# Constant tiles, second-layer weights and token transposes in the last stage of a four-stage transformer kernel

## The chip, the cores and the metric

The kernel runs on one core of one Trainium2 chip. The metric is the device time of one execution, in microseconds (us). Of the kernel before the change three runs are shown; the median counts.

A core has a matrix engine (TensorE, PE in the profile; its weight loads are PEld), a vector engine (VectorE, DVE), an activation engine (ScalarE, ACT), a general one (GpSimd, POOL), and a queue engine that here only issues DMAs (SyncE, SP). They run side by side; each executes its own instructions in order. SBUF is the memory on the core, with 128 partitions; PSUM is the matrix engine's output memory, here used as eight banks of 128 x 512 float32.

## What is computed

Two batches of 1024 tokens with 128 features pass four blocks in a row, each added to its input after a layer norm:

```python
x = x + _layernorm(_L0_attn_ref(_layernorm(x), Wq, Wk, Wv))      # 8 heads, full softmax attention
x = x + _layernorm(_L0_ffn_ref(_layernorm(x), ...))              # 8 experts, top 2, and a shared one
x = x + _layernorm(_L1_attn_ref(_layernorm(x), ...))             # 16 heads of 8, causal, ALiBi bias
x = x + _layernorm(_L1_ffn_ref(_layernorm(x), ...))              # two layers, below
```

The last block is a small transformer of its own, and the change lies in it. One layer of it (8 heads of 64, windows of 64 tokens, hidden size 341):

```python
h = shift_token(x)                 # second half of the features comes from the token before
q, k, v = jnp.split(h @ wqkv, 3, axis=-1)
q = l2norm(q) * qs
k = l2norm(k) * ksc
q, k = rotary_xpos(q, k)
o = local_attention(q, k, v)       # each window of 64 sees itself and the window before
x = x + o @ wo
h = shift_token(x)
h = (h - mu) / jnp.sqrt(var + 1e-05) * lg + lb
a, g = jnp.split(h @ w1 + b1, 2, axis=-1)
x = x + (a * jax.nn.gelu(g)) @ w2 + b2
```

## The kernel before

One function per block, `phase1` to `phase4`, written as generators. The tokens stay in SBUF in X, 16 tiles of 128 tokens (8 for each batch). Float32 products are made of halves: a value is split into a high and a low part (`split_r`, L214 and L215: a cast on ACT and a subtraction on DVE), and `mm3` (L49 to L51) multiplies them in three matmuls.

**What sets the order.** A framework with a planner compiles the program. The planner runs the program on a simulated timeline and gives each engine, whenever it comes free, the earliest instruction of the text that is ready there. PE alone is bound to the order of the text inside the fourth stage, by `in_line`, which chains its instructions. ACT's functions that need a table of their own (Ln, Exp, Gelu) are chained under the key "tables", and `k.last["tables"]` is the newest of them. `issue_after(ins)` puts what is written inside it behind `ins`; the third stage's `tick` enters it with four instructions, one each of ACT, DVE, SP and POOL.

**Third stage (`phase3`).** Steps of 4 heads by up to 512 queries by 128 keys. PE computes scores twice: in a pass ahead that only finds row maxima (L856, L860 on PE, L865 on DVE), and again (L891, L893) for the exponentials (L894, ACT, into pt). Of every second step pt is split into hl: a cast on ACT (L898) and a subtraction on POOL (L899). PE then multiplies pt or hl with V (L916, into pu). kz, the masked keys, is made on POOL (L836) and DVE (L838). The last token tiles go through L937 to L958 and the layer norm (L81 to L117) into X at L210.

**Preparation of the fourth stage.** From step m >= 54 on, each step of the third stage ends with `k.tick`, which runs `phase4` up to its next `yield`, behind the newest exponential, maximum, DMA and kz instruction. So the constants of pool p4c (`cp`: mask, identb, pick, away, fac), `normalize(0)` (the layer norm of batch 0 into F[0]: statistics on DVE at L81, L82 and L84, the power on POOL at L88, the application on DVE at L92), `weights(0)` and the first `stage_x` lie beside the third stage. `weights` loads a matrix through SP, scales it on POOL (L1041), casts it on ACT (L1043), subtracts on POOL (L1044), scales the rotary table on POOL in four parts (L1057) and a column (L1066).

**Fourth stage (`phase4`).** After "main" the pools p4e (`ep`, working tiles), p4w (`wp`) and p4s (`sp`) are opened. p4w holds F1 (batch 1), K0 to K4, V0 to V5, Vs0 to Vs5, xm, and the constants sh (the matrices that shift tokens), Z0 and Z1 (a zeroed pair of buffers into which half of q is cast), mz0 and mz1, and mT0 to mT2. They are filled at L1130 (sh, by SP), L1135 (mT, by three DMAs of POOL), L1137 and L1138 (memsets of Z and mz on POOL) and L1140 (the ones column of V). p4w lies where the third stage still has data: its first writes come after X's last write.

The work is 32 tiles of 128 tokens (2 layers x 2 batches x 8 tiles), in a software pipeline: round i of the loop does the steps of several tiles, in the order of

```python
for step in ("b0", "a2", "b2", "c2", "a", "e1", "d", "a1", "gated", "f", "x", "c", "gated", "e", "b1"):
```

each for tile i minus its lateness, (0, 0, 1, 2, 2, 2, 3, 4, 4, 4, 5, 6) for a, a1, a2, b0, b1, b2, c, c2, d, e, e1, f. What they do:

- x (every fourth round): `transposed` turns four token tiles into one PSUM bank (L221, PE), `split_r` splits it into hTh and hTl, the second half of the features shifted by one token, and at the first half of a batch the last column into xc.
- a: q and k by `mm3` from hTh and hTl into two banks; a square on ACT, the rotary products rot and t2 on DVE (L1174, L1177). a1: their sum on POOL (L1183), sums of squares (L1185, L1186). a2: the reciprocal norm on ACT and DVE.
- b0: q and k are scaled on POOL (L1208) and cast on ACT, q also into Z. b1: the low halves (L1222 DVE, L1223 POOL), and three transposing DMAs of SP: Z to Qz (L1229), k16 to K (L1230), q16 to Q (L1231). b2: v by `mm3` and its copy into V on ACT, then DMAs into Vs (L1245, L1247).
- c: high scores, the mask at L1258 and Qz times K at L1263, and the negated maximum into mz (L1272, DVE); ACT scales K into the next K (L1277). c2: mz transposed on PE (L1283) and copied to mT.
- d: mT and the scores (L1297, L1301, L1302), the exponential (L1303). e: PV (L1314) and the division (L1323, L1324). e1: transposes (L1331) and a copy (L1333). f: the output matrix (L1342) and the sum into F (L1343).
- g (the feed-forward part, several tiles at once): a generator, one part of which runs at each "gated".

Layer 2's `weights` are such a generator too; it is appended at i == 12, and uses pool p4v, opened at i == 2.

PSUM: one bank `ps_sm` (tile name sm), taken in turn by stage_x and stage_c2, and a ring of seven (tile name b, from three pools of 3, 3 and 1), which `bank()` goes round. `SRC` says for some steps whether they take the one or the other.

Of the kernel before, what the change touches and what calls it, by code (L numbers as in the profile page):

```python
# [10 lines left out]
F32 = mybir.dt.float32  # L11
F32R = mybir.dt.float32r
F16 = mybir.dt.float16
# [16 lines left out]
class Core:  # L30
# [7 lines left out]
    def pool(self, name, bufs, side, **kw):  # L38
        return self.tc.tile_pool(name=name, bufs=bufs, side=side, reuse_waits="tile", **kw)
# [956 lines left out]
def phase4(k, X):  # L996
# [5 lines left out]
    nc, A = k.nc, k.A  # L1002
    H, HD, HID = 8, 64, 341
    WS = 256.0
    with ExitStack() as es:
        pool = lambda name, bufs: es.enter_context(k.pool(name, bufs, "right"))
        cp = pool("p4c", 1)
        ps_sm = k.ps_sm
# [14 lines left out]
        fac = cp.tile([128, NT], F32, name="fac")  # L1023
        nc.sync.dma_start(fac, A["c_fac"])

        F = [cp.tile([128, NT, D], F32, name="F0")]

        def normalize(b):
            x = [X[:, NT * b + t, :] for t in range(NT)]
            mv, rstd = k.ln_stats(cp, lambda t: x[t])  # L1030
            yield
            k.ln_to(cp, [F[b][:, t, :] for t in range(NT)], lambda t: x[t], mv, rstd, scalar=b == 1)

        W = {}

        def weights(l, own, work):

            def split(pool, name, shape, dt, src, **kw):
                w = work(shape)
                nc.sync.dma_start(w, src)  # L1040
                nc.gpsimd.tensor_scalar(w, w, WS, None, ALU.mult)  # L1041
                h, lo = pool.tile(shape, dt, name=name + "h"), pool.tile(shape, dt, name=name + "l")
                nc.scalar.copy(h, w)  # L1043
                nc.gpsimd.tensor_tensor(lo, w, k.f(h) if dt == F32R else h, ALU.subtract)  # L1044
                return h, lo

            wq = split(own, "wq", [128, 1024], F16, A["L1_ffn_wqkv"][l][:, 0:1024])
            yield
            wv = split(own, "wv", [128, 512], F16, A["L1_ffn_wqkv"][l][:, 1024:1536])
            yield  # L1050

            qs = own.tile([128, 2, 2, HD], F32, name="qs")
            nc.sync.dma_start(qs, A["t_qks"][l].partition_broadcast(128))
            tab = own.tile([128, 4, NT, HD], F32, name="tab")
            nc.sync.dma_start(tab, A["c_rope"].rearrange("j (t p) d -> p j t d", p=128))
            for j in range(4):
                nc.gpsimd.tensor_tensor(tab[:, j], tab[:, j], qs[:, j // 2, j % 2, :].unsqueeze(1).to_broadcast([128, NT, HD]), ALU.mult)  # L1057
            yield
            wo = own.tile([128, 4, D], F32, name="wo")
            nc.sync.dma_start(wo, A["L1_ffn_wo"][l].rearrange("(a p) d -> p a d", p=128))  # L1060
            w2 = own.tile([128, 3, D], F32, name="w2")
            nc.sync.dma_start(w2, A["t_f2"][l])
            w1 = split(own, "w1", [128, 6, D], F16, A["t_f1"][l])
            col = own.tile([128, 9], F32, name="col")
            nc.sync.dma_start(col, A["t_col4"][l])
            nc.gpsimd.tensor_scalar(col[:, 0:3], col[:, 0:3], WS, None, ALU.mult)  # L1066
            W[l] = *wq, wo, *w1, w2, col, tab, *wv
# [3 lines left out]
        xc = [[cp.tile([128, 1], F16, name=f"xc{b}{n}") for n in "hl"] for b in range(B)]  # L1071
        late_half = slice(64, 128)

        def stage_x(l, b, c):

            hTh = cp.tile([128, 512], F16, name="hTh", bufs=2)
            hTl = cp.tile([128, 512], F16, name="hTl", bufs=2)
            ps = k.transposed(ps_sm, F[b], c)
            k.split_r(hTh[0:64, :], hTl[0:64, :], ps[0:64, :])
            k.split_r(hTh[late_half, 1:512], hTl[late_half, 1:512], ps[late_half, 0:511])  # L1080
            for h, x in zip((hTh, hTl), xc[b]):
                nc.scalar.copy(h[late_half, 0:1], x[late_half] if c else k.zero[late_half])
            if c == 0:
                k.split_r(xc[b][0][late_half], xc[b][1][late_half], ps[late_half, 511:512])
            S["h", l, b, c] = hTh, hTl
# [6 lines left out]
        yield from normalize(0)  # L1092
        yield from weights(0, cp, work0)
        stage_x(0, 0, 0)
        yield "main"

        ep = pool("p4e", 2)
        sq_place = k.acc.rearrange("p (j h) (e d) -> p j (h e) d", j=2, e=2)
        wp = pool("p4w", 1)
        F.append(wp.tile([128, NT, D], F32, name="F1"))  # L1100
        sp = pool("p4s", 2)
        ps = [es.enter_context(k.psum(f"p4{n}", b)) for n, b in zip("xyz", (3, 3, 1))]
# [11 lines left out]
                t = t.bitcast(F16)  # L1114
            return t[:, :shape[1]]
        from_sm = lambda shape, dt: ps_sm.tile(shape, dt, name="sm")
        SRC = {'c2': 0, 'f': 1, 'g': 1, 'x': 0}
        src_c2 = from_bank if SRC["c2"] else from_sm
        src_f = from_bank if SRC["f"] else from_sm
        src_g = from_bank if SRC["g"] else from_sm  # L1120
        src_x = FromBank if SRC["x"] else ps_sm
        QB = 3
        RV = 6
        RK = 5
# [1 line left out]
        V = [wp.tile([128, H, HD + 1], F32, name=f"V{i}") for i in range(RV)]  # L1126
        Vs = [wp.tile([128, H, HD + 1], F32, name=f"Vs{i}") for i in range(RV)]
        xm = [wp.tile([128, 64], F32, name=f"xm{b}") for b in range(B)]
        sh = wp.tile([128, 2, 128], F32, name="sh")
        nc.sync.dma_start(sh, A["c_shift"])  # L1130
        Z = [wp.tile([128, 4, 256], F16, name=f"Z{i}") for i in range(2)]
        mz = [wp.tile([128, 128], F16, name=f"mz{i}") for i in range(2)]
        mTs = [wp.tile([128, 128], F16, name=f"mT{i}") for i in range(3)]
        for m in mTs:
            nc.gpsimd.dma_start(m, A["c_rows4"][int(m is mTs[2])])  # L1135
        for i in range(2):
            nc.gpsimd.memset(Z[i], 0.0)  # L1137
            nc.gpsimd.memset(mz[i], 0.0)  # L1138
        for i in range(RV):
            nc.gpsimd.memset(V[i][:, :, HD : HD + 1], WS)  # L1140

# [5 lines left out]
        def cpy(n, dst, src, i=8):  # L1147
            (nc.scalar.copy if engine(n, i) == "a" else eng(n, i).tensor_copy)(dst, src)
# [52 lines left out]
        def stage_b0(i):  # L1201
# [11 lines left out]
            cpy("kh", ends(k16), pair4(kk), i)  # L1213
            cpy("z", ends(Z[i % 2]), pair4(q))
            S["b", i] = rot, q16, k16

        def stage_b1(i):
# [10 lines left out]
            fl = lambda ap: ap.rearrange("p a n -> p (a n)")  # L1228
            nc.sync.dma_start_transpose(Qz, fl(Z[i % 2]))  # L1229
            nc.sync.dma_start_transpose(K[k0][:, :, 64:192], fl(k16))  # L1230
# [105 lines left out]
        def stage_f(i):  # L1336
# [4 lines left out]
            for a in range(4):  # L1341
                nc.tensor.matmul(ps, oT[:, a, :], wo[:, a, :], start=a == 0, stop=a == 3)  # L1342
            nc.vector.tensor_tensor(F[b][:, t, :], ps, F[b][:, t, :], ALU.add)  # L1343

        def stage_g(l, b, t0, T, last):

            w1h, w1l, w2, col = W[l][3:7]
            x = F[b]
            g = slice(t0, t0 + T)
# [65 lines left out]
            for i in range(T):  # L1415
                nc.tensor.transpose(ps[:, i, :], yT[:, 128 * i : 128 * i + 128], k.ident)
            nc.vector.tensor_tensor(F[b][:, g, :], x[:, g, :], ps, ALU.add)
            if l == 1:
# [16 lines left out]
        gens = []  # L1435

        def advance():
            gens[:] = [g for g in gens if k.in_line(next, g, 0) is None]

        i = 0  # L1440
        while i < 32 + late[-1] or gens:
            if i == 4:
                gens.append(normalize(1))
            if i == 2:
                own = es.enter_context(k.pool("p4v", 1, "right"))
            if i == 12:
                gens.append(weights(1, own, lambda shape: ep.tile(shape, F32, name="t2")))
            for step in ("b0", "a2", "b2", "c2", "a", "e1", "d", "a1", "gated", "f", "x", "c", "gated", "e", "b1"):
                if step == "gated":
                    advance()  # L1450
                elif step == "x":
                    n = i - late[-1]
                    if n in ENDS:
                        l, b, t = where(n)
                        T = n - ([-1] + ENDS)[ENDS.index(n)]
                        gens.append(stage_g(l, b, t - T + 1, T, n >= LAST))
                    if i % 4 == 3 and i + 1 < 32:
                        l, b, t = where(i + 1)
                        k.in_line(stage_x, l, b, t // 4)
                else:  # L1460
                    j = names.index(step)
                    if 0 <= i - late[j] < 32:
                        k.in_line(stages[j], i - late[j])
            i += 1
# [3 lines left out]
def tile_kernel(ctx: ExitStack, tc: tile.TileContext, A, out, first=1, last=4):  # L1468
# [33 lines left out]
    k.exp_tables()  # L1502
    k.later = []
    gens = [f(k, X) for f in (phase1, phase2, phase3, phase4)[first - 1 : last]]
    ready = [False] * len(gens)

# [138 lines left out]
```

## Time and profile before

| | us |
|---|---|
| median of 3 runs | 1388.4 |
| lowest, highest | 1385.42, 1388.5 |
| the profiled execution | 1389.02 |
| its span, first to last instruction | 1387.2 |

| engine | busy us | share of the span |
|---|---|---|
| PE | 1159.8 | 84% |
| DVE | 1045.9 | 75% |
| ACT | 973.0 | 70% |
| POOL | 863.2 | 62% |

In the profiled execution L360, the first stage's attention, runs until 442 us; the third stage's score matmuls (L891) run until 991, X's last write (L210) ends at 1022.87, and the fourth stage's score matmuls (L1263) begin at 1029.4 and end at 1346.8. The granted clock of PE was 0.936 of full speed on average, and 0.54 between 1010 and 1040 us.

How to read the lines that follow. The chain of work that ended last is followed back from the last instruction, at each step to what released it; its rows give start, length, and engine, tile and line. "Issue" is time in which an engine waited for nothing that the profile shows. A timeline row gives start, length, engine, line, operation and tiles, output <- inputs, with partitions x elements and type; xN is the number of instructions in a row that are taken together, and the bracket is the engine's idle time before them and what ended it. A row of waits says who waited, for which instruction, for how long in all, how often, and the longest. DMA_DIRECT2D on POOL or SP is the issuing of a DMA, and DMA_TRANSPOSE that of a transposing one.

### The profile page before, as it was taken

Reading aid. Unit: us, or ns where it says so; the run is one execution under the profiler, and the core shown is the slowest. Engines: PE = TensorE matmul, PEld = TensorE weight load, DVE = VectorE, ACT = ScalarE, POOL = GpSimd, SP = SyncE. Lnnn points to the kernel's source line nnn. Section 1 sums busy time; section 2 is a strip of 40 time slices with the busy share of each in tenths; the row PEclk is TensorE's granted clock in tenths of the full one; section 3 lists DMA queues with packets and bytes.
Section 4 is the critical chain, followed back from the end, with each engine's and each line's share of the span. In section 5 each row is a group of like instructions: output and inputs, shape, how many; then the busy total and the mean of one; then the engine's idle time right before and its main releaser. Section 6 shows DMA issues by size and latency. Waiting matters only on the chain.

```text
span 1387.2 us, 28450 instructions
## 1 busy us (share of the span) xinstructions
PE 1159.8 (84%) x11534; PEld 729.5 (53%) x11534; DVE 1045.9 (75%) x2029; ACT 973.0 (70%) x1494; POOL 863.2 (62%) x536
## 2 busy tenths in 40 slices
PE   4789999999889687776998987689648888988986
PEld 1356666666556565544444443344325655655664
DVE  6776666876662688979978889775679887888854
ACT  2777777887667484641888876579757878887755
POOL 1666667777667363744576677576797786666611
PEclk7999999999999898987999999799959999999998
DMA  2000000010000211200000021000077755545530
GB/s 75 1 2 2 2 2 1 2 32 2 2 1 18 74 48 60 81 19 2 5 3 5 6 52 24 12 8 1 5 149 130 128 104 105 99 98 96 102 61 16
DMA packets 122530, 56.75 MB, mean 41 GB/s; under 512 B 105216, under 2 KB 114320, under 8 KB 122400
## 3 DMA queue, kind: packets, MB, share of 16 engines
q1 hardware_dynamic: 119920, 53.53, 18.3%
q8 instruction: 90, 1.47, 0.4%
q10 hardware_dynamic: 1472, 1.09, 0.3%
q0 software_dynamic: 1008, 0.33, 0.2%
q14 instruction: 40, 0.33, 0.1%
HBM read 20.99 MB, written 1.11 MB: 16 GB/s over the span
## 4 chain that ended last, share of the span: by engine, by line
PE 40%; DVE 31%; ACT 14%; POOL 6%; issue 6%; DMA 2%; SPq 0%; POOLq 0%; DVEq 0%; ACTq 0%
DVE mx L865 6%; PE big L360 5%; PE pu L49 4%; PE pu L51 3%; PE pu L50 3%; DVE nm L332 3%; ACT pt L894 2%; PE pu L916 2%; PE big L49 2%; PE big L50 2%; PE big L51 2%; DVE hl L642 1%; PE bankz L856 1%; PE bank L891 1%; DVE F L92 1%
## 5 line engine op out<-in xcount | busy, mean ns | idle before, releaser
L367 POOL TENSOR_TENSOR hl<-p,hl 128x1024 f16<-128x1024 f32 x128 | 273.9, 2143 | 139.0 <-ACT hl L366 110.9
L899 POOL TENSOR_TENSOR hl<-pt,hl 128x2048 f16<-128x2048 f32 (+1 forms) x48 | 164.7, 3435 | 102.3 <-ACT hl L898 58.9
L332 DVE TENSOR_REDUCE nm<-big 128x2 f32<-128x1024 f32 x128 | 155.1, 1219 | 31.9 <-PE big L329 31.1
L364 ACT ACTIVATE p<-big 128x1024 f32<-128x1024 f32 x128 | 130.8, 1022 | 51.9 <-PE big L360 51.1
L49 PEld LDWEIGHTS <-hl 128*128 128x128 f16 x1024 | 100.5, 98 | 73.8 <-DVE acc L392 41.2
L366 ACT CAST hl<-p 128x1024 f16<-128x1024 f32 x128 | 133.8, 1045 | 4.1
L865 DVE TENSOR_REDUCE mx<-bankz 128x1 f16<-128x512 f32 (+3 forms) x156 | 99.6, 657 | 26.3 <-PE bankz L860 19.5
L894 ACT ACTIVATE pt<-bank 128x512 f32<-128x512 f32 (+1 forms) x173 | 97.3, 601 | 26.0 <-PE bank L893 11.8
L865 DVE TENSOR_REDUCE mx<-bank 128x1 f16<-128x512 f32 (+1 forms) x148 | 94.4, 654 | 18.2 <-PE bank L860 12.5
L1208 POOL TENSOR_TENSOR rot<-rot,rn 128x512 f32<-128x512 f32 x64 | 66.9, 1066 | 61.8 <-DVE rn L1198 44.8
L49 PE MATMUL pu<-V1h,hl 128*128 128x129 f16 x512 | 92.6, 224 | 12.4 <-DVE acc L392 11.1
L50 PEld LDWEIGHTS <-hl 128*128 128x128 f16 x1024 | 101.2, 99 | 0.0
L49 PE MATMUL pu<-V0h,hl 128*128 128x129 f16 x512 | 92.8, 224 | 9.2 <-DVE acc L392 7.5
L51 PEld LDWEIGHTS <-hl 128*128 128x128 f16 x1024 | 100.3, 98 | 0.0
L894 ACT ACTIVATE pt<-bankz 128x512 f32<-128x512 f32 (+1 forms) x131 | 75.2, 597 | 35.8 <-PE bankz L893 29.4
L1183 POOL TENSOR_TENSOR rot<-rot,t 128x512 f32<-128x512 f32 x64 | 83.9, 1321 | 15.6 <-DVE t L1177 12.2
L50 PE MATMUL pu<-V0l,hl 128*128 128x129 f16 x512 | 92.1, 221 | 0.0
L51 PE MATMUL pu<-V0h,hl 128*128 128x129 f16 x512 | 92.1, 222 | 0.0
L51 PE MATMUL pu<-V1h,hl 128*128 128x129 f16 x512 | 92.0, 222 | 0.0
L50 PE MATMUL pu<-V1l,hl 128*128 128x129 f16 x512 | 92.0, 221 | 0.0
L898 ACT CAST hl<-pt 128x2048 f16<-128x2048 f32 (+1 forms) x48 | 78.4, 1634 | 10.1 <-PE pu L916 9.8
L891 PE MATMUL bank<-qst,kz 128*128 128x512 f16 (+3 forms) x222 | 66.7, 344 | 14.8 <-DVE mx L865 9.4
(418 smaller groups left out, 3797.9 us busy)
## 6 DMA issues: line engine op xcount, KB each, us to landing
sb<-sd SPq DMA_DIRECT2D x16, 512.0 KB, 4.1
Vs<-V SPq DMA_DIRECT2D x60, 130.0 KB, 2.4
work<-in_t_w SPq DMA_DIRECT2D x3, 512.0 KB, 3.6
out<-F SPq DMA_DIRECT2D x3, 256.0 KB, 2.3
X<-in_L_attn_x SPq DMA_DIRECT2D x2, 256.0 KB, 3.4
w<-in_t_wqk SPq DMA_DIRECT2D x1, 512.0 KB, 4.8
wv<-in_t_wv ACTq DMA_DIRECT2D x1, 512.0 KB, 3.7
X<-in_L_attn_x ACTq DMA_DIRECT2D x1, 512.0 KB
```

The source lines that it names most:

```text
L49: mm(out, lh, rh, start=start, stop=False, **kw)
L50: mm(out, lh, rl, start=False, stop=False, **kw)
L51: mm(out, ll, rh, start=False, stop=stop, **kw)
L332: S["red"] = nc.vector.tensor_reduce(S["n", u][:, i // 2, c, :], ps, AX.X, ALU.max, negate=True)
L364: S["exp"] = nc.scalar.activation(p, st, AF.Exp, scale=QSCALE**-2)
L366: nc.scalar.copy(hl[:, 0], p)
L367: S["lo"] = nc.gpsimd.tensor_tensor(hl[:, 1], p, hl[:, 0], ALU.subtract)
L865: S["max"] = nc.vector.tensor_reduce(out, ps[:, :, :n], AX.X, ALU.max, negate=True)
L891: nc.tensor.matmul(st[:, a, :w], kz[:, a0 + a, 128 * j : 128 * j + 128], q1[:, s : s + w], start=True, stop=not diag)
L894: S["exp"] = nc.scalar.activation(pt[:, a0 : a0 + m, :w], st[:, :, :w], AF.Exp)
L899: nc.gpsimd.tensor_tensor(hl[:, 1, :, :w], pt[:, :, :w], hl[:, 0, :, :w], ALU.subtract)
L1183: eng("ra" if j else "rb", i).tensor_tensor(rot[:, j], rot[:, j], t2[:, j], ALU.add)
```

## The change

Three edits, all in `phase4`:

1. sh, Z, mz and mT move from p4w to p4c, and the instructions that fill them move from behind "main" into the preparation, right behind the constant fac and ahead of `normalize(0)`. They take 6,400 bytes of each partition (1,024 + 2 x 2,048 + 2 x 256 + 3 x 256); p4e's tiles move by as much.
2. Layer 2's `weights` are wrapped in `later`, which runs each part inside `issue_after` of the newest table instruction.
3. stage_x takes its bank from the ring (`SRC["x"]` is 1 and `places[0]` is `FromBank`); only the first stage_x, in the preparation, still uses ps_sm.

```diff
--- before
+++ after
@@ -1023,6 +1023,16 @@
         fac = cp.tile([128, NT], F32, name="fac")
         nc.sync.dma_start(fac, A["c_fac"])
 
+        sh = cp.tile([128, 2, 128], F32, name="sh")
+        nc.sync.dma_start(sh, A["c_shift"])
+        Z = [cp.tile([128, 4, 256], F16, name=f"Z{i}") for i in range(2)]
+        mz = [cp.tile([128, 128], F16, name=f"mz{i}") for i in range(2)]
+        mTs = [cp.tile([128, 128], F16, name=f"mT{i}") for i in range(3)]
+        for m in mTs:
+            nc.gpsimd.dma_start(m, A["c_rows4"][int(m is mTs[2])])
+        for i in range(2):
+            nc.gpsimd.memset(Z[i], 0.0)
+            nc.gpsimd.memset(mz[i], 0.0)
         F = [cp.tile([128, NT, D], F32, name="F0")]
 
         def normalize(b):
@@ -1071,11 +1081,13 @@
         xc = [[cp.tile([128, 1], F16, name=f"xc{b}{n}") for n in "hl"] for b in range(B)]
         late_half = slice(64, 128)
 
+        places = [ps_sm]
+
         def stage_x(l, b, c):
 
             hTh = cp.tile([128, 512], F16, name="hTh", bufs=2)
             hTl = cp.tile([128, 512], F16, name="hTl", bufs=2)
-            ps = k.transposed(ps_sm, F[b], c)
+            ps = k.transposed(places[0], F[b], c)
             k.split_r(hTh[0:64, :], hTl[0:64, :], ps[0:64, :])
             k.split_r(hTh[late_half, 1:512], hTl[late_half, 1:512], ps[late_half, 0:511])
             for h, x in zip((hTh, hTl), xc[b]):
@@ -1114,11 +1126,11 @@
                 t = t.bitcast(F16)
             return t[:, :shape[1]]
         from_sm = lambda shape, dt: ps_sm.tile(shape, dt, name="sm")
-        SRC = {'c2': 0, 'f': 1, 'g': 1, 'x': 0}
+        SRC = {'c2': 0, 'f': 1, 'g': 1, 'x': 1}
         src_c2 = from_bank if SRC["c2"] else from_sm
         src_f = from_bank if SRC["f"] else from_sm
         src_g = from_bank if SRC["g"] else from_sm
-        src_x = FromBank if SRC["x"] else ps_sm
+        places[0] = FromBank if SRC["x"] else ps_sm
         QB = 3
         RV = 6
         RK = 5
@@ -1126,16 +1138,6 @@
         V = [wp.tile([128, H, HD + 1], F32, name=f"V{i}") for i in range(RV)]
         Vs = [wp.tile([128, H, HD + 1], F32, name=f"Vs{i}") for i in range(RV)]
         xm = [wp.tile([128, 64], F32, name=f"xm{b}") for b in range(B)]
-        sh = wp.tile([128, 2, 128], F32, name="sh")
-        nc.sync.dma_start(sh, A["c_shift"])
-        Z = [wp.tile([128, 4, 256], F16, name=f"Z{i}") for i in range(2)]
-        mz = [wp.tile([128, 128], F16, name=f"mz{i}") for i in range(2)]
-        mTs = [wp.tile([128, 128], F16, name=f"mT{i}") for i in range(3)]
-        for m in mTs:
-            nc.gpsimd.dma_start(m, A["c_rows4"][int(m is mTs[2])])
-        for i in range(2):
-            nc.gpsimd.memset(Z[i], 0.0)
-            nc.gpsimd.memset(mz[i], 0.0)
         for i in range(RV):
             nc.gpsimd.memset(V[i][:, :, HD : HD + 1], WS)
 
@@ -1437,6 +1439,14 @@
         def advance():
             gens[:] = [g for g in gens if k.in_line(next, g, 0) is None]
 
+        def later(steps):
+
+            while True:
+                with k.tc.issue_after(k.last["tables"]):
+                    if next(steps, steps) is steps:
+                        return
+                yield
+
         i = 0
         while i < 32 + late[-1] or gens:
             if i == 4:
@@ -1444,7 +1454,7 @@
             if i == 2:
                 own = es.enter_context(k.pool("p4v", 1, "right"))
             if i == 12:
-                gens.append(weights(1, own, lambda shape: ep.tile(shape, F32, name="t2")))
+                gens.append(later(weights(1, own, lambda shape: ep.tile(shape, F32, name="t2"))))
             for step in ("b0", "a2", "b2", "c2", "a", "e1", "d", "a1", "gated", "f", "x", "c", "gated", "e", "b1"):
                 if step == "gated":
                     advance()

```

## The prediction

> **What bounds the kernel now.** I read the chain of work that ended last first, as shares of the span, because no engine is busy all the time:
>
> ```profile
> PE 40%; DVE 31%; ACT 14%; POOL 6%; issue 6%; DMA 2%; SPq 0%; POOLq 0%; DVEq 0%; ACTq 0%
> ```
>
> PE and DVE carry 71% of it in turn; POOL, busy for 62% of the span, carries 6%. So time on POOL counts only where the chain passes through it, and two such places lie where the change works. The same chain in order of time (start, length, what) shows both:
>
> ```profile
> 853.64 2.52 POOL acc L1041
> 856.38 3.81 POOL tab L1057 x4
> 861.52 6.57 POOL hl L899 x2
> 871.26 12.87 DVE F L92 x8
> ...
> 1022.90 0.87 DVE ln_st L81 x4
> 1024.09 3.88 DVE ln_rs L84
> 1028.00 0.69 DVE rot L1174
> ```
>
> The first four are the fourth stage's preparation inside the third stage; the last three are the hand-over from third stage to fourth. There PE stands longest. Its waits from 1000 us on (for what, total, times, longest):
>
> ```profile
> PE b L1263 <- DMA Qz<-Z: 15.0, 1, 15.0
> PE sm L1283 <- DVE hTl L215: 8.5, 3, 3.2
> PE sm L1283 <- DVE xc1l L215: 7.1, 2, 3.8
> ```
>
> The first is a score matmul that waits for the first transposed Qz; the other two are stage_c2, which waits until the bank that stage_x filled has been read. POOL's timeline says what stands before Qz:
>
> ```profile
> 1022.92 1.73 POOL L1135 DMA_DIRECT2D mT<-in_c_rows  x3
> 1024.62 1.00 POOL L1137 MEMSET Z<- 128x1024 f16 x1
> 1025.51 0.25 POOL L1138 MEMSET mz<- 128x128 f16 x1
> 1025.65 1.00 POOL L1137 MEMSET Z<- 128x1024 f16 x1
> 1026.54 0.25 POOL L1138 MEMSET mz<- 128x128 f16 x1
> 1026.69 0.34 POOL L1140 MEMSET V<- 128x8 f32 x6
> ```
>
> All of this starts only after X's last write (L210, DVE, until 1022.87): the new tiles of p4w lie where the third stage still had data.
>
> **Constant tiles, at the hand-over.** Seven POOL instructions leave: from 1022.92 to 1026.69, 3.77 us. On SP the sh DMA leaves (0.57 us at 1020.07, ahead of the K transposes at 1020.73). Three engines stand behind POOL here. DVE's L84 takes 3.88 us, against a median of 0.17 for that line, and ends as POOL gets through this run: 3.71 could go. ACT's two Z casts waited 0.27 and 0.41 us for the memsets, then Qz started at 1026.29. PE's L1263 began at 1029.43; with Z ready early it would wait for K instead, whose first transpose had landed when ACT read it at 1024.15, so PE could start at about 1024.2: 5.2 earlier. What is late next is K and the V copies, which stay in p4w behind L210. Of 3.77, 3.71 and 5.2 the path takes what its slowest member gives; POOL's own later work (L1241, L1225, L88 at 1028.06) moves by 3.77. I take **−3.8**; bounds 0 (another POOL run stands in front of L84) and −5.2.
>
> A rule weighs against this. L84 lasted past seven POOL instructions, not one. The Trainium skill ("SBUF — State Buffer", section "SBUF: two separate sides") says that a GpSimd and a VectorE instruction lock their shared port for one whole instruction, and whoever starts first goes first; L84 would then have waited for the one memory clear or DMA in progress, some 0.6 us as an estimate, and the DVE share of the gain would be 0.6. The row shows the longer wait, so I go by the row.
>
> **Constant tiles, in the third stage.** The same instructions (1.73+1.00+0.25+1.00+0.25 = 4.23 us gross, 3.77 from start to start) and SP's sh DMA (0.57) now stand next to the preparation's first ones. POOL's timeline there:
>
> ```profile
> 850.61 0.65 POOL L1011 DMA_DIRECT2D mask<-in_c_mask  x1
> ...
> 853.02 0.54 POOL L1021 DMA_DIRECT2D away<-in_c_away  x1
> 853.64 2.76 POOL L1041 TENSOR_SCALAR acc<-acc 128x1024 f32<-128x1024 f32 x1
> 856.38 4.94 POOL L1057 TENSOR_TENSOR tab<-tab,qs 128x512 f32<-128x512 f32 x4
> 861.50 8.07 POOL L899 TENSOR_TENSOR hl<-pt,hl 128x2048 f16<-128x2048 f32 x2
> ...
> 893.23 2.12 POOL L899 TENSOR_TENSOR hl<-pt,hl 128x1024 f16<-128x1024 f32 x1 [10.27 <-ACT hl L898]
> ```
>
> From 844.87 to 882.98 POOL has no gap, and L899 at 861.50, whose ACT half was ready at 848.1, stands 13.4 us behind the preparation. Queued behind it are PV matmuls (L916 waited 2.60 us for it) and the exponentials, which wait 7.38 us for its buffers. If the new instructions go ahead of it, the chain pays up to 4.2. Against that, POOL then idles 10.27 us, which takes the 3.77 whole, and what a planner that gives each engine the earliest ready instruction of the text pushes back first is the later ticks' L1041 and L1057 (7.7 us), which nobody reads in that stretch. The bounds are 0 and +4.2; I take **+1.0**, a quarter, as the idle row is the larger. SP's extra 0.57 us costs nothing: SP issues little there, and sh is first read after the fourth stage starts.
>
> Three of the moved instructions are POOL DMAs, and VectorE runs at the same time. POOL's own three in this stretch took 0.65, 0.54 and 0.54 us, like the three at the hand-over (0.58 on average). The same page and section of the Trainium skill warns that VectorE can starve such a DMA's descriptors, about 620 ns growing to about 3100; three of those would put some 7.4 us on POOL, as an estimate. The rows show no such growth.
>
> The move also shifts p4e by 6,400 bytes, so the first rot tiles come to lie over the third stage's last kz buffer. Its last reader, L891, ends at about 991.4; the first write, stage_a's L1174, came at 991.54 and had waited for PE anyhow. Cost 0, and 0.4 at most if that reader slips. p4w's tiles wait for L210 as before.
>
> **Second layer's weights.** The wrapper orders instructions behind the newest table instruction. The third stage's tick passes four such instructions, one for each engine, so I read it as an order within one engine, here ACT. ACT's weight casts (L1043) were at 1113.25, 1116.62 and 1125.25, behind a table instruction already. The layer's early work is on SP (qs, tab, wo, w1 and col DMAs, 998.15 to 1011.8) and on POOL (L1057 and L1066, 1016.95 to 1022.97), which it would not hold: **0**. If it did hold them, those 5.95 us would leave POOL just before the hand-over and come back at about 1115, in a steadier stage. Bounds −5.95 and +5.95.
>
> **Token transposes in the ring.** Today stage_x and stage_c2 share one bank, and c2 waits at 1067.36, 1103.60, 1148.14, 1191.40, 1234.20 and 1276.56 for stage_x's last reader: 8.5+7.1+1.2 = 16.8 us in all. In the ring x's bank is used again seven allocations later (c, c, g, e, e, b2, a), by the next stage_a. That stage reads hTh and hTl, which the same reader writes, so nearly all of the wait shifts from c2 to a, a few instructions on. What goes is c2 itself and the first matmuls, which now run inside the wait: about 0.5 us in each of six places, 3.0. Against it, each bank of the ring is claimed one step sooner after a stage_x; at i=7 c's second bank would come 0.4 us late (t2's read ended at 1061.37, c began at 1060.97). I take **−2.0**. Bounds: −16.8 if all waits go; +10.5 if the new order holds up a step before c2 by 1.75 us, half of the 3.2 to 3.8 of the longest waits, in each of six rounds.
>
> **Sum.** −3.8 + 1.0 + 0 − 2.0 = −4.8. The profiled execution took 1389.02 us (span 1387.2 and 1.8 around it), 0.6 above the median of 1388.4 (1385.42 to 1388.5). So 1384.2 for it, 1383.6 against the median.
>
> **Rivals.**
> - The third stage takes back what the hand-over gives: the chain runs through POOL there, so +3.8 replaces +1.0. −2.0 in all: 1386.4. For it: POOL carries 13 us of the chain; against: the 10.27 us of idle.
> - The weights do leave the hand-over. POOL is then free from about 1017, and −5.95 comes on top: 1377.7. Against it: the code names one ACT instruction.
> - **Slower**: a DVE instruction starves in the third stage. L92's first one took 10.89 us (871.26 to 882.15; the other seven 0.33 each) while POOL ran without a gap, and it carries the chain. If the longer POOL run holds a second DVE instruction (L92, L84 or L838) as long, that is +10.9, with the full 4.2: −3.8 + 4.2 − 2.0 + 10.9 = +9.3, 1397.7; with half such a stall 1392.3. It decides from a stall of about 5.8 us on, where the sum passes +4.2. Against it: L1057 and L899 already run as densely, with one such stall only.
> - The edits change nothing measurable because all waits shift on: near 1388; it goes with the first rival.
>
> **How the numbers follow.** This kernel's measurement can tell about 0.3%, 4.2 us, from no change: borders at 1384.2 and 1392.6. Forecast 1383.6: 0.39, faster. Third stage takes it back: 0.30, same. Weights leave: 0.09, faster. Starved DVE instruction (or the ring's +10.5): 0.22, slower. So faster 0.48, same 0.30, slower 0.22. The forecast's own range is 1380 to 1386. The range reaches down to 1377, below the weights' case, and up to 1394, inside the slower case, and leaves out some 0.15 above and 0.05 below.
>
> **What would show it.** Right: no L1135, L1137 or L1138 near 1023 us; L84 at about 0.2 us; the wait for Qz at 10 us or less; the memsets near 853; L899 at 861.5 to 865.7; stage_c2's waits on L215 gone, and shorter ones at stage_a's L49; the second layer's L1057 still near 1017. Wrong: L1057 gone from there (second rival); L899 late by the full 4 us with PE waiting behind it (first); a second DVE row of 5 us or more between 850 and 890 (third).

## The result, and the profile after

The changed kernel takes 1405.6 us (median of 4 runs, 1405.2 to 1406.1) against 1388.5 us before; the ratio is 1.0122, with a 95% interval of 1.0096 to 1.0148. It is 17 us, or 1.2%, slower. The forecast was 4.8 us faster, and the time lies above the range.

The profiled execution of the changed kernel has a span of 1403.4 us, 16.2 over the one before. Cut at landmarks that both have, it shows where (us; "POOL 25" is the end of POOL's 25th L899, at 830 us, up to which both programs are the same):

| stretch | before | after | difference |
|---|---|---|---|
| start to POOL 25 | 830.2 | 832.8 | +2.6 |
| to the third stage's last score matmul (L891) | 161.3 | 170.0 | +8.8 |
| to X's last write (L210) | 31.4 | 36.1 | +4.7 |
| to the first score matmul of the fourth stage (L1263) | 6.6 | 1.4 | -5.2 |
| to the first sum into F (L1343) | 24.2 | 25.1 | +0.9 |
| to the last sum into F | 311.5 | 314.9 | +3.3 |
| to the end | 22.1 | 23.2 | +1.1 |

The first row is no effect: the same instructions took 830.2 to 836.2 us in the profiles of this study. The fourth row is the gain that was forecast at the hand-over. It is outweighed by the two rows above it. The 3.3 us of the sixth row go with the clock granted to PE in that stretch, 0.96 against 0.98: PE was busy there for 275.1 us against 269.2.

The chain of work that ended last, first as shares, then in order of time from 876 us on:

```profile
PE 41%; DVE 33%; ACT 12%; POOL 7%; issue 5%; DMA 2%; SPq 0%; POOLq 0%; DVEq 0%; ACTq 0%
```

```profile
876.29 11.94 DVE F L92 x8
...
922.12 2.54 DVE mx L865 x4
924.68 3.87 DVE mx L870
...
948.97 3.81 DVE ao L945
...
1025.27 4.22 POOL tab L1067 x4
...
1030.59 4.50 POOL rot L1210 x4
...
1038.24 0.70 DVE X L210
```

Of before's four rows in the preparation only L92 is left in the chain. The row maxima (L865, L870) carry much of it from 913 to 931, and at the hand-over POOL's queue does: the second layer's table multiply (now L1067) and four L1210 stand in front of the last layer norm's L88 and so of X's last write. L84's 3.88 us are gone, as forecast. Two of the rows are VectorE instructions that take far longer than elsewhere in this profile, L870 3.87 us (0.23 at 866.24) and L945 3.81 (0.29 at 902.11); each ends as the L899 that runs beside it on POOL does.

What the fills did to POOL's own order in the third stage (timeline):

```profile
856.16 1.60 POOL L1032 DMA_DIRECT2D mT<-in_c_rows  x3
857.72 1.00 POOL L1034 MEMSET Z<- 128x1024 f16 x1
859.67 4.11 POOL L899 TENSOR_TENSOR hl<-pt,hl 128x2048 f16<-128x2048 f32 x1
```

L899 did not move back. Seen from POOL 25 it begins 4.4 us earlier than before, and the weights' scaling and the table multiply stand behind it. The planner has drawn up the rest of the stage anew, on all engines. In the compiled order, the fills left out, 671 instructions of PE and 245 of DVE's 2,029 stand at another place than before. What PE waits for between POOL 25 and the last score matmul, before:

```profile
PE sm L221 <- DVE F L92: 9.2, 1, 9.2
PE bank L891 <- DVE mx L865: 4.6, 7, 3.3
PE bank L856 <- DVE mx L865: 2.9, 5, 1.2
PE bankz L891 <- DVE mx L865: 2.0, 5, 0.8
PE bankz L856 <- DVE mx L865: 1.5, 6, 0.6
```

and after:

```profile
PE bankz L856 <- DVE mx L865: 9.3, 4, 8.5
PE bankz L891 <- DVE mx L865: 6.3, 9, 2.5
PE bank L891 <- DVE mx L865: 5.4, 10, 3.3
PE bank L856 <- DVE mx L865: 4.2, 5, 1.9
PE sm L221 <- DVE F L92: 1.5, 2, 0.9
```

The waits for DVE's maxima, which read the banks that PE fills next, grow from 11.0 to 25.2 us; the wait for L92 falls by 7.7. But the longest of them, 8.5 us, is L92 again: the maximum that this matmul waits for stands behind the eight L92 in DVE's queue, as the chain shows:

```profile
876.29 11.94 DVE F L92 x8
888.23 0.48 DVE mx L865
888.75 0.59 PE bankz L856
```

So the two kinds belong together: PE's waits for maxima and L92 grow from 20.2 to 26.7 us, by 6.5, where the stretch grows by 8.8. PE's own wait for POOL, 3.2 us for L899 before, is gone.

In the fourth stage PE's longest waits are these:

```profile
PE b L1265 <- POOL K L1227: 18.4, 1, 18.4
PE sm L1285 <- DVE mz L1274: 13.5, 10, 2.4
PE b L49 <- ACT hTh L214: 7.1, 4, 2.0
```

The first score matmul waits for a memset of K behind X's last write, no longer for Qz. The 16.8 us that c2 waited for stage_x's last reader are gone. In their place stage_a waits 7.1 us for hTh, and c2's wait for mz is 5.2 longer than before (13.5 against 8.3).

### The profile page after: what moved, and what is told of

The parts are those of the page before. It is cut to its first block, busy times and chain, and to the rows that moved or that the text cites. A ratio compares the mean times of both kernels' runs of the same rounds, so it can differ in the third digit from the quotient of the medians.

```text
span 1403.4 us, 28453 instructions
## 1 busy us (share of the span) xinstructions
PE 1168.2 (83%) x11534; PEld 733.4 (52%) x11534; DVE 1049.1 (75%) x2029; ACT 972.2 (69%) x1494; POOL 859.1 (61%) x536
## 4 chain that ended last, share of the span: by engine, by line
PE 41%; DVE 33%; ACT 12%; POOL 7%; issue 5%; DMA 2%; SPq 0%; POOLq 0%; DVEq 0%; ACTq 0%
DVE mx L865 7%; PE big L360 4%; PE pu L49 4%; PE pu L51 3%; PE pu L50 3%; DVE nm L332 3%; PE pu L916 3%; PE big L49 2%; PE big L50 2%; PE big L51 2%; POOL rot L1210 2%; ACT pt L894 2%; DVE hl L642 1%; POOL rot L1185 1%; PE bank L891 1%
## 5 line engine op out<-in xcount | busy, mean ns | idle before, releaser
L899 POOL TENSOR_TENSOR hl<-pt,hl 128x2048 f16<-128x2048 f32 (+1 forms) x48 | 164.7, 3435 | 108.4 <-ACT hl L898 76.0
L865 DVE TENSOR_REDUCE mx<-bankz 128x1 f16<-128x512 f32 (+3 forms) x156 | 99.9, 658 | 27.6 <-PE bankz L860 22.3
L894 ACT ACTIVATE pt<-bank 128x512 f32<-128x512 f32 (+1 forms) x173 | 97.1, 596 | 28.2 <-PE bank L893 12.6
L865 DVE TENSOR_REDUCE mx<-bank 128x1 f16<-128x512 f32 (+1 forms) x148 | 94.3, 656 | 21.0 <-PE bank L856 11.3
L1210 POOL TENSOR_TENSOR rot<-rot,rn 128x512 f32<-128x512 f32 x64 | 66.3, 1058 | 59.6 <-DVE rn L1200 50.7
L898 ACT CAST hl<-pt 128x2048 f16<-128x2048 f32 (+1 forms) x48 | 78.3, 1631 | 12.1 <-PE pu L916 11.8
L891 PE MATMUL bank<-qst,kz 128*128 128x512 f16 (+3 forms) x222 | 66.3, 343 | 15.9 <-DVE mx L865 10.0
```

What stands on the lines that cost most here:

```text
L865: S["max"] = nc.vector.tensor_reduce(out, ps[:, :, :n], AX.X, ALU.max, negate=True)
L894: S["exp"] = nc.scalar.activation(pt[:, a0 : a0 + m, :w], st[:, :, :w], AF.Exp)
L899: nc.gpsimd.tensor_tensor(hl[:, 1, :, :w], pt[:, :, :w], hl[:, 0, :, :w], ALU.subtract)
L1210: eng(en, i).tensor_tensor(rf[:, r, :], rf[:, r, :], rn[:, r].unsqueeze(2).to_broadcast([128, H, HD]), ALU.mult)
```

## The experiments

Theory, after this profile: the loss comes from the **order** that the planner chose, once seven instructions more stood on POOL in the preparation. Rival: it comes from their **load**, the 4 us that they take there. A second rival is the **ring**. The table has all runs; the stretches are those above, from the profiled execution of each.

| run | median, us | ratio to before (95%) | POOL 25 to L891 | to L210 | to L1263 | to first F | to last F |
|---|---|---|---|---|---|---|---|
| the change | 1405.6 | 1.0122 (1.0096 to 1.0148) | 170.0 | 36.1 | 1.4 | 25.1 | 314.9 |
| part1_alone | 1404.3 | 1.0107 (1.0088 to 1.0125) | 173.0 | 35.4 | 2.4 | 24.6 | 312.6 |
| part3_alone | 1393.8 | 1.0035 (1.0022 to 1.0049) | 158.3 | 30.4 | 7.9 | 28.5 | 312.0 |
| held_constants | 1394.1 | 1.0038 (1.0021 to 1.0056) | 157.8 | 29.6 | 6.3 | 29.6 | 314.8 |
| layer2_held | 1390.1 | 1.0008 (0.9994 to 1.0022) | 158.1 | 28.7 | 7.8 | 23.1 | 320.2 |
| fills_old_order | 1391.9 | 1.0020 (1.0009 to 1.0030) | 161.9 | 31.4 | 5.9 | 23.4 | 312.9 |
| order_without_fills | 1406.2 | 1.0119 (1.0105 to 1.0133) | 169.6 | 40.0 | 3.2 | 25.7 | 313.2 |
| change_old_order | 1388.2 | 0.9997 (0.9987 to 1.0006) | 162.0 | 31.4 | 5.9 | 23.4 | 308.9 |
| fills_in_idle_slot | 1389.4 | 1.0000 (0.9987 to 1.0013) | 161.0 | 31.9 | 5.9 | 23.4 | 312.7 |
| ring_old_order | 1387.1 | 0.9989 (0.9975 to 1.0004) | 158.3 | 31.4 | 6.5 | 24.3 | 311.0 |
| smallest_fill | 1396.4 | 1.0057 (1.0038 to 1.0076) | 158.4 | 29.7 | 6.3 | 28.2 | 314.6 |
| fills_end_of_preparation | 1393.5 | 1.0036 (1.0023 to 1.0050) | 161.8 | 34.8 | 1.4 | 24.8 | 315.5 |
| new_order_pe_as_before | 1392.7 | 1.0034 (1.0014 to 1.0053) | 161.7 | 34.8 | 1.4 | 26.3 | 313.4 |
| new_order_dve_as_before | 1392.8 | 1.0031 (1.0013 to 1.0048) | 165.6 | 31.7 | 1.4 | 25.7 | 313.4 |
| table_later | 1403.1 | 1.0093 (1.0068 to 1.0118) | 171.7 | 33.0 | 2.2 | 25.1 | 312.4 |
| hand_over_by_hand | 1383.5 | 0.9962 (0.9947 to 0.9978) | 157.7 | 31.9 | 1.1 | 26.1 | 311.0 |

With before's order, the stretch from POOL 25 to L891 took 157.7 to 162.0 us. Before's own profile is among the long ones: PE's granted clock was 0.88 there, against 0.90 to 0.91 in the eight other runs with this order, and PE was busy for 128.7 us against 125.0 to 126.8. So a difference of some 3 us to before's profile tells nothing in that column. Five of the eight took 157.7 to 158.3 us (part3_alone, held_constants, layer2_held, ring_old_order, hand_over_by_hand); they are called the short ones below.

**The parts.** Part 2 needed no run: with the wrapper and without it the order of instructions is the same on all five engines, in the kernel before, with part 1, and with parts 1 and 3. Parts 1 and 3 were run by themselves.

```diff
 part1_alone: sh, Z, mz, mT and their fills behind fac, as in the change; SRC["x"] stays 0
 part3_alone: SRC["x"] is 1 and places[0] is FromBank, as in the change; the constants stay in p4w
```

> Part 1 alone: the constant tiles in p4c, filled in the preparation; weights and ring as before. Theory (third stage): the third stage's rest, from the preparation on, is laid out in another order and loses 8 to 9 us, the last layer norm loses 4 to 5 more, and the hand-over gives about 5 back: 8 to 16 us slower than before, nearly all of the whole change's +17. Rival (ring): the third stage's loss is small for this part alone, and half or more of the +17 comes with the ring: below +8 us here. If it gains, as predicted, -2.8.

> Part 3 alone: stage_x takes its bank from the ring; the constant tiles as before. The prediction's step: -2 us, with stage_c2's waits on the split gone. Theory (third stage): within 3 us of before, as the third stage's order is unchanged up to its last transposes. Rival (ring): +8 us or more, since each ring bank is claimed a step sooner in every fourth round.

Part 1 has nearly the whole loss: 15.5 us by the medians, with 11.8 in the third stage. Part 3 loses 5 us: no gain of 2, more than the theory's 3, less than the ring rival's 8, and not where the ring is at work, for the rounds of the fourth stage take as long as before (312.0). It is the hand-over (66.8 us from L891 to the first F, against 62.2), where the planner put other instructions side by side. A VectorE instruction that has 0.3 us in the run fills_old_order took 5.5 in part3_alone (DVE's timeline, then POOL's):

```profile
1028.45 5.53 DVE L114 SCALAR_TENSOR_TENSOR ln_nb<-ln_mv,ln_rstd 128x8 f32<-128x8 f32 x1 [0.83 <-POOL ln_rstd L88]
```

```profile
1028.36 1.18 POOL L1225 TENSOR_TENSOR k<-rot,k 128x512 f16<-128x512 f32 x1
1029.47 2.49 POOL L1185 TENSOR_TENSOR rot<-rot,t 128x512 f32<-128x512 f32 x2
1031.91 2.03 POOL L1210 TENSOR_TENSOR rot<-rot,rn 128x512 f32<-128x512 f32 x2
```

It ends when POOL's run ends, at 1033.9. L84 takes 0.18 us in this run: the stall that left L84 has found L114.

**Nothing in the third stage.** `third` holds the third stage's last instructions of POOL and SP.

```diff
 held_constants: the tiles in cp; their fills stay behind "main", in
+        for e in ("Pool", "SP"): held.enter_context(k.tc.issue_after(third[e]))
 layer2_held: the kernel before, and around each part of weights(1)
+        for e in ("Activation", "Pool", "SP"): held.enter_context(k.tc.issue_after(newest(e)))
```

> The constant tiles lie in p4c as in the change, but their fills are held behind the third stage's last instruction of POOL and of SP, so nothing of them stands in the third stage; weights and ring as before. Theory (third stage): the order of the third stage stays that of before, and the hand-over's gain remains: 3 to 5 us faster than before. Rival (the tiles' new place costs, by moving p4e): as slow as the change or at least not faster than before.

> The kernel before, but the second layer's weight preparation is held on ACT, POOL and SP alike, behind the newest instruction of each, so that its table multiply (5.4 us of POOL) can't stand at the hand-over. If that multiply delays the hand-over, as the prediction's second rival had it: 3 to 6 us faster. If it only fills POOL's idle time: within 2 us; if its late place costs as much at the second layer's start: slower by up to 6.

held_constants keeps the third stage's order and loses nothing there, but it isn't faster: 5 us slower, with L114 at 3.1 us and 5.4 more between the first score matmul and the first F. So the theory's second half, that the hand-over's gain stays once the third stage is spared, failed. layer2_held does what the wrapper's words say: the table multiply now begins at 1131. From the last score matmul to the first F its profile gains 2.5 us (59.7 against 62.2), and by its runs it is no faster than the kernel before. Its rounds are 8.7 us longer in this profile, but that execution was the slowest of 11 (1396.9 us, median 1390.1), with a clock of 0.94 in the rounds against 0.98 before; only the 4.9 us that come at one place, between the sums of tiles 9 and 10, where the second layer's first tile enters, look like a price of the late multiply, and that is not shown apart from the clock.

**Order against load.** After all of the program is written, each engine's instructions are tied in the order of a list; lines from there on are one higher.

```diff
+        for names in ORDER.values():      # one list for each of the five engines
+            for x, y in zip(names, names[1:]):
+                k.tc.add_manual_dep(named[y], x, dep, reason="order")
```

For fills_old_order the list is the order of the kernel before, with the seven fills behind the away DMA and sh's behind fac; change_old_order adds the ring, and fills_in_idle_slot has them at 883 us instead. order_without_fills has the order that the planner gave part 1, with the fills behind the last L899. ring_old_order is part 3 under the order before.

> Part 1's move alone, with the order of the kernel before laid down by hand on all five engines: the seven fills stand on POOL behind the away DMA and the shift DMA on SP behind fac, everything else stands exactly as before. So only their work is added to the third stage. Order theory (the loss comes from the planner's new order, not from the fills' own time): third stage 0 to 4 us longer, hand-over 3 to 5 shorter, in all 5 us faster to 1 us slower than before. Load theory (4 us more on a full POOL push the exponentials and PE back): third stage 8 us or more longer, in all 8 to 15 us slower, like part 1 alone.

> The reverse: the order that the planner chose for part 1 alone is laid down by hand on all five engines, but the fills are taken out of the third stage and stand on POOL behind its last subtraction. Order theory: the third stage is as long as in part 1 alone (12 us over kernels with the old order), in all 12 to 18 us slower than before. Load theory: the third stage is back within 3 us, in all at most 5 us slower.

> The whole change (tiles moved, stage_x in the ring; the weights' wrapper alters nothing) under the order of the kernel before, laid down by hand. Order theory: the prediction's sum was right but for the new order, so 6 us faster to 1 us slower. Ring rival: the ring's banks hold the fourth stage up whatever the order, so at least 4 us slower than the same kernel without the ring.

> As the first of these, but the seven fills stand in POOL's idle slot of 10.3 us at 883 to 893, under the old order. If the hand-over's gain is real: third stage unchanged, in all 3 to 5 us faster than before. If a VectorE instruction is kept waiting there anyway, a later one in place of L84, as in the run with held constants (L114, 3.1 us): within 2 us of before.

> Part 3 alone (stage_x in the ring) under the order of the kernel before, laid down by hand on all five engines. Order theory: the ring itself gives 2 to 4 us, as the prediction's step said, and part 3 alone lost 5 us only by the planner's new order at the hand-over: 2 to 4 us faster than before. Ring rival: as slow as part 3 alone, 5 us slower than before.

The two first runs settle most of it. The new order without the fills there costs 8.3 us in the third stage against before's profile, 11 to 12 against the five short ones, and the kernel is as slow as the change. The fills' work under the old order costs less, but not nothing. The stretch is only 0.6 us longer than in before's profile, which had the lower clock; against the five short profiles it is some 4 us longer. L899 begins 3.8 us later, the fills' length, and the PV matmuls wait that much longer for it, before (first row) and in fills_old_order:

```profile
PE pu L916 <- POOL hl L899: 3.2, 3, 2.6
PE pu L917 <- POOL hl L900: 7.2, 3, 6.6
```

That wait is 7.5 us in change_old_order and 3.1 to 3.5 in the runs with the old order and no early fills. By its runs fills_old_order is 3.5 us slower than before, where the order theory allowed 1: right on the third stage, wrong on the sum. Load theory's 8 us or more did not come. fills_in_idle_slot, with the fills where POOL idles, is as fast as before: within the 2 us of its second case, though not by that case's reason, for L114 took 0.34 us there.

The whole change under the old order is as fast as the kernel before. The ring rival falls with change_old_order, which is 3.7 us faster than the same without the ring; alone the ring gave 1.7, just short of the 2 to 4 expected, with an interval that includes no change.

Why the gain of 5 us at the hand-over shrank to 0.7 under the old order is seen on ACT (fills_old_order):

```profile
1025.70 1.07 ACT L1149 COPY V<-b 128x512 f32<-128x512 f32 x2 [1.33 <-DVE X L211]
1026.66 0.73 ACT L1278 ACTIVATE K<-K,fac 128x512 f16<-128x512 f16 x1
1027.29 0.61 ACT L1149 CAST k<-rot 128x512 f16<-128x512 f32 x1
1027.79 1.14 ACT L1149 CAST Z<-rot 128x512 f16<-128x512 f32 x2
```

The casts into Z, whose buffer has been ready since the third stage, stand behind copies into V, which is in p4w and waits for X's last write. With the fills out of the way, ACT's order was late next.

**Other draws of the order.**

```diff
 smallest_fill: only memset(mz[0]) and memset(mz[1]) in the preparation; the rest as in held_constants
 fills_end_of_preparation: all fills behind "yield from weights(0, cp, work0)"
```

> Of the seven fills only the two memsets of mz (0.5 us of POOL in all) stand in the preparation, with the planner's own order; the other five are held behind the third stage's last instruction of POOL and SP. If the loss goes with the time that is added to POOL: the third stage is at most 1 us longer. If any new instruction on POOL makes the planner draw up the rest of the third stage anew, and that is what costs: its length differs from that of kernels with the old order by several us either way, with no relation to the 0.5 us.

> All fills stand in the preparation, but behind the first layer's weights instead of ahead of batch 0's layer norm, with the planner's own order. The same work on POOL as in part 1 alone, and an order of its own. If the loss comes from the work: as slow as part 1 alone, 12 to 18 us. If from the order that happens to be chosen: another time, which can lie anywhere from 5 us faster to 20 us slower; no theory gives its sign.

The same seven instructions, a little further down the text, take 161.8 us in the third stage instead of 173.0. So the loss does not go with the work alone. Two memsets of 0.5 us give another order again, and this one costs the third stage nothing (158.4): that is what was expected if the loss goes with the time added, so this run does not speak for the order. Its 4 us more from the first score matmul to the first F go with L114 again, 5.31 us long there; the rest of the 7.6 us that it loses is not explained.

**Which engine, and the last layer norm.** For the first two only one engine's list is laid down (and the fills' place on POOL and SP); table_later has part 1's own order, but layer 2's table multiply behind batch 1's L88, and the last layer norm's L88 ahead of two L1208.

```diff
 new_order_pe_as_before:  ORDER holds PE alone
 new_order_dve_as_before: ORDER holds DVE alone
 table_later: in ORDER["Pool"], L1057 x4 and L1066 moved from ahead of L1208, L88 to behind the next L88
```

> Part 1 alone with the fills where the change has them, but PE's order as in the kernel before, laid down by hand; DVE, ACT and most of POOL and SP are left to the planner. If PE's new order (maxima's matmuls ahead of scores, so that PE stands for the reductions) is what costs: the third stage (from the 25th subtraction on POOL at 830 us to the last score matmul) takes 158 to 162 us instead of 173. If DVE's new order costs: still 169 or more.

> The same with DVE's order as before and PE's left to the planner. If PE's order costs: the third stage takes 169 us or more. If DVE's: 158 to 162. If either engine's old order pulls the others' back with it, both runs are short, and then the two can't be told apart.

> Part 1 alone with the order that the planner chose for it, laid down by hand, but for POOL at the hand-over: the second layer's table multiply and column (5.7 us) stand behind the L88 of batch 1's layer norm, and the last layer norm's L88 ahead of the two L1208 that it stood behind. If POOL's queue in front of that L88 is what holds the last layer norm: the time from the last score matmul to X's last write falls from 35 us to 30 or 31, and the whole is 3 to 5 us faster than part 1 alone. If another engine holds it: within 1.5 us of part 1 alone. The third stage stays at 169 to 173.

With PE's order alone the third stage is back at 161.7 us, though 156 instructions of DVE and 146 of ACT stand at other places than before; PE's waits for maxima and L92 are back at 20.1 us. With DVE's alone it is 165.6, between the two answers: some of PE's order came back with it (416 instructions stand at other places than before, against 649 in part 1). So PE's order carries most of the loss. That DVE's adds to it isn't excluded. Stretched VectorE instructions as such are not the cause: DVE was busy in the stretch for 114.5 us before and 117.3 after, but for 118.2 in new_order_pe_as_before, whose stretch is 161.7.

table_later did not do what was expected. The way to X's last write is 33.0 us, 2.4 of 4.1 back and not the 30 or 31 forecast, and by the medians it is 1.2 us faster than part 1, with overlapping intervals. Still, the table sorts the runs: where the second layer's table multiply stands ahead of the last layer norm's L88 on POOL (the change, part1_alone, order_without_fills, fills_end_of_preparation, new_order_pe_as_before), the stretch to L210 takes 34.8 to 40.0 us; where it stands behind, 28.7 to 33.0, in the kernel before and in all other runs. Both speak for the multiply as part of that loss, no more than that; where the rest comes from stays open.

**A faster version.** The old order by hand, the ring, the fills at 883 us, and ACT's casts into Z ahead of what waits for X:

```diff
 hand_over_by_hand: fills_in_idle_slot with the ring, and in ORDER
   Activation: both casts into Z ahead of the last layer norm's L117
   SP: the first Qz and K, K ahead of the third tile's Q
   Pool: the memsets of Vs and K ahead of those of V
```

> The old order laid down by hand, stage_x in the ring, the fills in POOL's idle slot of the third stage, and three edits of that order at the hand-over: ACT's first two casts into Z stand ahead of the last layer norm instead of behind the copies into V; SP's first Qz and the two K transposes stand ahead of the third tile's Q; POOL's memsets of K and Vs stand ahead of those of V. If the hand-over's gain of 5 us was lost to ACT's order, the first score matmul starts within 2.5 us of X's last write instead of 5 to 6.6, and the kernel is 5 to 9 us faster than before. If another engine is late instead: 2 to 4 us faster, what the ring alone gives.

The first score matmul starts 1.1 us after X's last write, as expected if ACT's order was what held it, and the kernel takes 1383.5 us, 5.3 less than before and 22 less than the change: the only run whose interval lies wholly below 1. Of the 5.5 us gained there, 1.9 go until the first F. The edits on ACT, SP and POOL were made together, so their shares aren't told apart.

## Why the prediction was wrong

- **Constant tiles, in the third stage: +1.0. This step failed.** It took the order of the stage as given, with the fills in a gap or ahead of L899, and let the planner push back only "the later ticks' L1041 and L1057". What came instead is a new order of all engines: 8.8 us in the third stage, mostly by PE's order and its waits for DVE, and 4.7 up to X's last write. With the fills taken out of the stage that order still cost 8.3 us, so this is no cost of the moved instructions. The term was also too small for what it did count: under the old order the PV matmuls wait 4.0 us longer for L899, nearly the bound of +4.2. A quarter was taken because POOL idles for 10.27 us later on, but PE waits for L899 before that idle time comes. No rival had the new order. The slower one named a second starved DVE instruction of 5 us or more between 850 and 890 us, and there is none (L92's eight take 11.9 us in all, 12.9 before); two shorter ones, L870 and L945 with some 3.6 us too much each, lie later on the chain, and what they add to the loss isn't shown apart. The three mT DMAs took 1.60 us there, 1.73 at the hand-over: they did not grow.
- **Constant tiles, at the hand-over: -3.8.** In size it came: -5.2 us from X's last write to the first score matmul, 0.9 of it given back up to the first F. The bound of -5.2 for PE was the right one. But it depends on the order of ACT, whose Z casts stand ahead of the V copies in the changed kernel; under the old order only 0.7 is left, since I had put ACT's Z casts down as waiting for the memsets alone, not for the queue ahead of them.
- **Second layer's weights: 0.** Right: the program is the same. The second rival's price for really holding them (5.95 us) was too high: layer2_held gained 2.5 us up to the first F in its profile and nothing by its runs.
- **Ring: -2.0.** Right in sign under the old order (-3.7, and -1.7 with an interval that includes no change), and the waits shifted from c2 to stage_a as described. Under the planner's order for part 3 alone it loses 5 us, at the hand-over, where L114 is stretched; the sum had no term for that.
- **The range** had no case in which the order itself costs 13 us; the slower case ended at +9.3.

## What to carry to other kernels

Where a planner orders the engines, an instruction added early is charged not only its own time but a new draw of everything behind it, which can be worth more. Before a sum of moved microseconds is believed, the order with the edit and without it has to be compared engine by engine; where it differs, the old order laid down by hand shows what the edit itself is worth, and is the place to improve from. And where a wait is taken away, look at what stands ahead in the same engine's queue before counting the gain.

## What the runs showed of the hardware

- A VectorE instruction next to an unbroken run on POOL can wait far longer than one POOL instruction: L92 10.9 us past four of them in the kernel before, L114 5.5 us past five. But in held_constants four L92 in a row took 2.2, 2.2, 2.2 and 4.1 us there, one POOL instruction each, 10.6 in all. The rule of the Trainium skill ("SBUF — State Buffer", section "SBUF: two separate sides") that the shared port goes to whoever starts first, for one whole instruction, fits the second and not the first; what decides between them stays open.
- The clock granted to PE differed between profiles with the same order of the third stage: from POOL 25 to the last score matmul it was 0.88 in the kernel before, where PE was busy for 128.7 us, and 0.90 to 0.91 in eight others, where it was busy for 125.0 to 126.8. A difference of 3 us between two single profiles can be the clock alone.
